# A graph network on one core: the first sort reads its partner keys in place, and the table's tiles are evacuated a step later

## The chip, the core and the metric

The kernel runs on one core of a Trainium2 chip. A core has TensorE (PE) for matrix products and transposes, VectorE (DVE), ScalarE (ACT) and GpSimd (POOL) for element-wise work, SyncE (SP) as a queue for DMAs, and 16 DMA engines. Each engine works through its own instructions in the order in which they were written down and waits for others by semaphores. SBUF is the working memory, PSUM the memory into which TensorE writes. The metric is the device time of the whole kernel in microseconds. Three runs took 4322.46, 4323.11 and 4330.8 us; the median is 4323.11 us.

## The reference: what is computed

There are 12500 nodes with 256 features each and 200000 edges, sorted by destination. The first layer normalises the features, multiplies them by a weight matrix, gathers a row of the product for each edge and adds it, times the edge's weight, to the edge's source node. The second layer is attention over the edges with 8 heads.

```python
h = relu(layernorm(x))
# layer 0: table = h @ W0 ; out[src] += edge_weight * table[dst]
x = x + segment_sum(edge_weight[:, None] * (h @ weight)[dst], src, 12500)
h = relu(layernorm(x))
# layer 1: q, k, v = projections of h; softmax of q[dst].k[src] over the edges of one dst
x = x + segment_sum(attn * v[src], dst, 12500) @ Wo.T + bo
```

## The kernel before

The edges come sorted by destination, while layer 0 adds up by source. So the kernel sorts them again on the chip. The edges are split into three blocks of 128 x 512 edges and a rest of seven groups of 512. A block's keys (source and destination packed in one 32-bit number) are a tile K of 128 x 512, and the edge weights are a tile of values (V in the code, `W` in the profile). `sort(b)` is a bitonic sort of one block, written as a generator that yields after each stage. A stage compares two halves of the keys: `a` and `c` are views of K, the lower and upper partner of each pair. It makes a mask m of 128 x 256 (L231), the minimum (L234) and the maximum (L235) into a new K, and moves the values by predicated copies with the mask (L241, or L238 and L239 in a stage that flips one half). All five are on VectorE. Ahead of them ScalarE copies the partner keys `c` into a PSUM tile kp (L224) and all values into a PSUM tile vp (L229). There are 129 stages in the first sort. In 6 of them the partner is another tile, just transposed by TensorE (`kp=kt`); the other 123 make the copy kp.

Block 0 is sorted alone, before any layer-0 sum can start. Beside it runs `hidden()`, a second generator, which makes the table HW = relu(layernorm(x)) @ W0, 98 tiles of 128 rows in chunks of four. For one tile the functions are stats (DVE, L561 and L562), root (ACT, L569, once per chunk), scale (DVE, L575 and L576, once per chunk), norm (GpSimd, L581), turn (PE transposes, L587), turned (ACT, L592, PSUM to SBUF), mult (PE, L598) and put (ACT, L604, PSUM to SBUF, and after four tiles the store of the chunk to HW by SP, L607). The list `fs` gives for each function the lag in steps behind stats, and its order is the order in which a step's instructions are written into the engines' queues. A chunk of x is loaded by SP (L541) when the chunk before it is at its second tile; three chunks have buffers.

The loop that joins the two is in `layer0`. In each step s it advances the sort by a stage, then hidden by a step. In step 3 it prepares the rest block. From step 18 it loads what the seven rest groups need, and after step 20 it advances `group_l0`, which builds one-hot matrices on DVE (L495 to L507), multiplies on PE (L511, L518), evacuates on ACT (L513, L519), and adds rows to a table in DRAM by indirect DMAs from GpSimd (L522). Two fills a step, 20 copies of a part of x into the first accumulator (L734) and five small zero rows (L1470), go out on SP until they are used up. The order on all engines is as written, by `manual_schedule`.

PSUM tiles that matter: `pt` has one buffer (turn writes it, turned frees it); `bank()` gives `pg` with two buffers, which mult, and in a rest group the one-hot product and both message products, share.

After the loop `load_s` gathers rows of HW by the sorted destinations dT (L285 makes dT on DVE, L630 is the gather on GpSimd), and the rest of layer 0, the other two sorts and layer 1 follow.

Of the kernel before, what the change touches and what calls it, by code (L numbers as in the profile page):

```python
# [64 lines left out]
def sblk(g):  # L65
    b = 0
    while g >= GS[b]:
        g -= GS[b]
        b += 1
    return b, g  # L70
# [7 lines left out]
class Gnn:  # L78
# [127 lines left out]
    def sort(self, b):  # L206
# [3 lines left out]
        def halves(v, flip):  # L210
            return v[:, :, 0], v[:, ::-1, 1] if flip else v[:, :, 1]

        def stage(d, flip=False, kp=None, vp=None, rows=False):
            nonlocal K
            e = d if rows else G // (2 * d)
            n = G // (2 * e)

            def pairs(t):
                return t.rearrange("p (n c m) -> p n c m", c=2, m=e)

            a, c = halves(pairs(K), flip)
            if kp is None:
                kp = tp.tile([P, G], F32, name="kp", bufs=1)[:, :G // 2].rearrange("p (n m) -> p n m", m=e)
                nc.scalar.copy(kp, c)  # L224
            else:
                kp = halves(pairs(kp), flip)[1]
            if vp is None:
                vp = tp.tile([P, G], F32, name="vp", bufs=1)
                nc.scalar.copy(vp, V)  # L229
            m = wp.tile([P, G // 2], I32, name="m").rearrange("p (n m) -> p n m", m=e)  # L230
            nc.vector.tensor_tensor(m, a, kp, op=ALU.is_gt)  # L231
            K = wp.tile([P, G], F32, name="K")
            lo, hi = halves(pairs(K), flip)
            nc.vector.tensor_tensor(lo, a, kp, op=ALU.min)  # L234
            nc.vector.tensor_tensor(hi, a, kp, op=ALU.max)  # L235
            v, p = pairs(V), pairs(vp)
            if flip:
                nc.vector.copy_predicated(v[:, :, 0], m, p[:, ::-1, 1])  # L238
                nc.vector.copy_predicated(v[:, ::-1, 1], m, p[:, :, 0])  # L239
            else:  # L240
                nc.vector.copy_predicated(v, m[:, :, None, :].to_broadcast([P, n, 2, e]), p[:, :, ::-1])  # L241
# [7 lines left out]
        for k in range(1, 10):  # L249
            stage(1 << (k - 1), True)  # L250
            yield
            for j in range(k - 2, -1, -1):
                stage(1 << j)
                yield
# [271 lines left out]
    def hidden(self):  # L526
        nc, wp, tp = self.nc, self.wp, self.tp
        nt = (N + P - 1) // P
        X, Y, T, M, R = {}, {}, {}, {}, {}
        nch = (nt + HC - 1) // HC  # L530
        chunks = list(range(nch - 2, nch)) + list(range(nch - 2))
        seq = [i for c in chunks for i in range(c * HC, min(nt, (c + 1) * HC))]

        def rows(t, c):
            n = min(HC * P, N - c * HC * P) // P
            return t[c * HC * P:(c * HC + n) * P].rearrange("(k p) d -> p k d", p=P), n

        def load(c):
            X[c] = wp.tile([P, HC, D], F32, name="xh", bufs=3)
            v, n = rows(self.i["x"], c)  # L540
            nc.sync.dma_start(X[c][:, :n], v)  # L541
            if N - (c * HC + n) * P < P and n < HC:
                nc.sync.dma_start(X[c][:N % P, n], self.i["x"][N - N % P:N])

        def tile_of(i):
            return divmod(i, HC) + (min(P, N - i * P),)

        def last(i):
            return i % HC == HC - 1 or i == nt - 1

        def stats(i):
            c, j, r = tile_of(i)
            if j == 0:
                M[c] = wp.tile([P, HC, 2], F32, name="mv4")
                if nt - c * HC <= HC:
                    nc.vector.memset(M[c], 1.0)
            k = chunks.index(c) + 1
            if j == 1 and k < nch:
                load(chunks[k])
            st = wp.tile([P, 6], F32, name="st")  # L560
            nc.vector.bn_stats(st[:r], X[c][:r, j])  # L561
            nc.vector.bn_aggr(M[c][:r, j], st[:r])  # L562
            T[i] = {}

        def root(i):
            c, j, r = tile_of(i)
            if last(i):
                R[c] = wp.tile([P, HC, 2], F32, name="sd4")
                nc.scalar.activation(R[c][:, :j + 1, 0], M[c][:, :j + 1, 1], AF.Sqrt, bias=self.eps)  # L569

        def scale(i):
            c, j, r = tile_of(i)
            if last(i):
                m, a = M[c][:, :j + 1], R[c][:, :j + 1]
                nc.vector.reciprocal(a[:, :, 0], a[:, :, 0])  # L575
                nc.vector.scalar_tensor_tensor(a[:, :, 1], m[:, :, 0], -1.0, a[:, :, 0], op0=ALU.mult, op1=ALU.mult)  # L576

        def norm(i):
            c, j, r = tile_of(i)
            h = T[i]["h"] = wp.tile([P, D], F32, name="h", bufs=3)  # L580
            nc.gpsimd.tensor_scalar(h[:r], X[c][:r, j], R[c][:r, j, 0:1], R[c][:r, j, 1:2], op0=ALU.mult, op1=ALU.add)  # L581

        def turn(i):
            r = tile_of(i)[2]
            pt = T[i]["pt"] = tp.tile([P, G], F32, name="pt", bufs=1)[:, :D].rearrange("p (k e) -> p k e", e=P)
            for k in range(2):
                nc.tensor.transpose(pt[:, k, :r], T[i]["h"][:r, k * P:(k + 1) * P], self.ident[:r, :r])  # L587

        def turned(i):
            r = tile_of(i)[2]  # L590
            ht = T[i]["ht"] = wp.tile([P, 2, P], F32, name="ht", bufs=3)
            nc.scalar.activation(ht[:, :, :r], T[i]["pt"][:, :, :r], AF.Relu)  # L592

        def mult(i):
            r = tile_of(i)[2]
            ph = T[i]["ph"] = self.bank()[:, :D]
            for k in range(2):
                nc.tensor.matmul(ph[:r], T[i]["ht"][:, k, :r], self.w0[:, k], start=(k == 0), stop=(k == 1))  # L598

        def put(i):  # L600
            c, j, r = tile_of(i)
            if j == 0:
                Y[c] = wp.tile([P, HC, D], F32, name="yh")
            nc.scalar.copy(Y[c][:r, j], T.pop(i)["ph"][:r])  # L604
            if j == HC - 1 or i == nt - 1:
                v, n = rows(self.HW, c)
                nc.sync.dma_start(v, Y[c][:, :n])  # L607
                if r < P:
                    nc.sync.dma_start(self.HW[N - r:N], Y[c][:r, n])

        load(chunks[0])
        q = HC + 1
        fs = ((turn, q + 1), (mult, q + 2), (norm, q), (scale, 1), (stats, 0), (root, 0), (turned, q + 1), (put, q + 2))
        for s in range(nt + q + 2):
            for f, k in fs:
                if 0 <= s - k < nt:
                    f(seq[s - k])
            yield
# [839 lines left out]
    def layer0(self):  # L1458
        tc, nc = self.tc, self.nc
        ET = mybir.EngineType  # L1460
        with tc.tile_pool(name="k0", bufs=1) as self.k0, tc.tile_pool(name="w0", bufs=2) as self.wp, \
# [23 lines left out]
            def fills(n):  # L1485
                for _ in range(n):
                    if fill:
                        fill.pop(0)()

            with tc.manual_schedule(engines={ET.SP, ET.PE, ET.DVE, ET.Activation, ET.Pool}):  # L1490
# [7 lines left out]
                s, gs, live = 0, [], None  # L1498
                while rest or live:
                    for f in list(rest):  # L1500
                        if next(f, self) is self:
                            rest.remove(f)
                    if s == 3:
                        self.prep_a(NPT)
                        self.prep_c(NPT)
                    if s == 18:
                        for g in range(NS, NS + 2):
                            self.load_l0(g)
                        gs = list(range(NS, NG))
                    if s > 20:  # L1510
                        if live is None and gs:
                            g = gs.pop(0)
                            live = self.group_l0(g)
                        if live is not None and next(live, self) is self:
                            live = None
                            if gs and gs[0] + 1 < NG:
                                self.load_l0(gs[0] + 1)
                    if s > 0:
                        fills(2)
                    s += 1  # L1520
# [7 lines left out]
                for t in range(NGS + 6):  # L1528
                    b, p = sblk(t) if t < NGS else (NPT, t - NGS)
# [130 lines left out]
```

## Time and profile before

| what | value |
|---|---|
| median of three runs | 4323.11 us |
| the profiled execution | 5571.24 us, of it a span of 5569.2 us |
| PE busy | 3863.3 us, 69% |
| DVE busy | 3443.4 us, 62% |
| POOL busy | 2921.8 us, 52% |
| ACT busy | 2172.3 us, 39% |
| mean granted TensorE clock | 0.819 of full speed |
| first gather of HW starts | 403.06 us after the start |

Times in the profile are of one execution with the profiler on. A row of the costliest groups gives line, engine, operation, the tiles written and read, their shapes, the count, the busy time and the mean duration in ns. A row of the timeline gives start and duration in us, and in brackets how long the engine had stood idle before it and who released it. The view of waits gives total, count and longest in us. A busy-time row of a stretch gives the busy microseconds of PE, of its weight loads, of DVE, ACT and POOL, then the granted clock, the mean busy share of the DMA engines and GB/s.

The costliest rows of the page that belong to sort and table:

```profile
L241 DVE COPY_PREDICATED W<-m,vp 128x512 f32<-128x512 int32 x317 | 229.7, 725 | 0.0
```

### The profile page before, as it was taken

Reading aid. Unit: us, or ns where it says so; the run is one execution under the profiler, and the core shown is the slowest. Engines: PE = TensorE matmul, PEld = TensorE weight load, DVE = VectorE, ACT = ScalarE, POOL = GpSimd, SP = SyncE. Lnnn points to the kernel's source line nnn. Section 1 sums busy time; section 2 is a strip of 40 time slices with the busy share of each in tenths; the row PEclk is TensorE's granted clock in tenths of the full one; section 3 lists DMA queues with packets and bytes.
Section 4 is the critical chain, followed back from the end, with each engine's and each line's share of the span. In section 5 each row is a group of like instructions: output and inputs, shape, how many; then the busy total and the mean of one; then the engine's idle time right before and its main releaser. Section 6 shows DMA issues by size and latency. Waiting matters only on the chain. (4 is left out here: it accounts for less than half of the span.)

```text
span 5569.2 us, 61840 instructions
## 1 busy us (share of the span) xinstructions
PE 3863.3 (69%) x14078; PEld 2557.5 (46%) x14078; DVE 3443.4 (62%) x7373; ACT 2172.3 (39%) x6027; POOL 2921.8 (52%) x3096
## 2 busy tenths in 40 slices
PE   4745677656667577777477767777777777677776
PEld 3532344334434344444255555555555555455554
DVE  7786777557666355555265556556666666566665
ACT  4452334223323122222144444444454444455453
POOL 2316655555555565666445555555555555555552
PEclk8777788778788799999677878788888888888888
DMA  6424456555555566666556666666676776666673
GB/s 180 96 66 141 146 164 181 167 161 162 164 157 168 156 201 197 201 194 192 173 172 196 190 199 203 201 193 206 197 213 208 208 214 208 201 207 210 202 213 105
DMA packets 627547, 1004.38 MB, mean 180 GB/s; under 512 B 97274, under 2 KB 450359, under 8 KB 627165
## 3 DMA queue, kind: packets, MB, share of 16 engines
q0 software_dynamic: 196224, 596.49, 38.0%
q1 hardware_dynamic: 430941, 403.79, 22.9%
q8 instruction: 119, 1.95, 0.2%
q14 instruction: 263, 2.15, 0.1%
HBM read 788.60 MB, written 224.47 MB: 182 GB/s over the span
## 5 line engine op out<-in xcount | busy, mean ns | idle before, releaser
L960 POOL DMA_INDIRECT kvt<-KV,ci x1564 | 1495.4, 956 | 1321.8 <-DVE pv L1059 666.3
L630 POOL DMA_INDIRECT hg<-HW,dT x1384 | 1311.5, 948 | 977.0 <-issue 369.3
L993 PE MATMUL pq<-qt,oht 80*128 80x256 f32 x3128 | 898.8, 435 | 395.5 <-issue 175.1
L650 PE MATMUL pg<-hg,ohs 128*128 128x256 f32 x2768 | 923.1, 454 | 134.4 <-issue 92.7
L994 DVE TENSOR_TENSOR pr<-pq,kvt 128x512 f32<-128x512 f32 x782 | 517.3, 686 | 796.2 <-remote 505.1
L1071 PE MATMUL pg<-pv,oh 128*82 128x264 f32 x3126 | 945.0, 455 | 67.6 <-DVE pv L1059 44.6
L993 PEld LDWEIGHTS pq<-qt,oht 80*128 80x128 f32 x3128 | 675.2, 220 | 564.4 <-issue 260.4
L650 PEld LDWEIGHTS pg<-hg,ohs 128*128 128x128 f32 x2768 | 549.6, 219 | 495.9 <-issue 370.9
L977 ACT ACTIVATE oh<-iof,nsl 128x82 f32<-128x82 f32 x1564 | 437.1, 350 | 855.5 <-remote 564.1
L1071 PEld LDWEIGHTS pg<-pv,oh 128*82 128x82 f32 x3126 | 556.4, 182 | 359.6 <-issue 163.0
L639 DVE TENSOR_SCALAR ohs<-iop,sT,eT 128x128 f32<-128x128 f32 x1384 | 473.2, 404 | 123.7 <-remote 74.8
L1059 DVE TENSOR_TENSOR pv<-kvt,pp 128x1024 f32<-128x1024 f32 x391 | 471.4, 1206 | 63.2 <-ACT pb L1048 43.5
L995 DVE TENSOR_REDUCE sim<-pr 128x32 f32<-128x1024 f32 x391 | 477.1, 1220 | 13.4
L649 PE MATMUL pg<-wn,cs 128*1 128x256 f32 x746 | 254.4, 427 | 196.5 <-ACT wn L671 73.1
L968 ACT ACTIVATE oht<-slt,npcol 80x512 f32<-80x512 uint8 x391 | 282.1, 722 | 257.2 <-remote 102.1
L671 ACT COPY wn<-pg 128x256 f32<-128x256 f32 x373 | 138.0, 370 | 384.0 <-PE pg L650 131.1
L465 ACT ACTIVATE sd<-mv,eps 128x1 f32<-128x1 f32 x128 | 37.7, 294 | 600.0 <-DVE sd L470 279.1
L697 PE MATMUL tps<-wkv,ht 128*128 128x512 f32 x512 | 262.5, 639 | 0.0
L969 ACT ACTIVATE oht<-oht 80x512 f32<-80x512 f32 x391 | 246.4, 630 | 12.4
L438 PE MATMUL pt<-w,ht 128*128 128x256 f32 x304 | 115.9, 468 | 173.5 <-ACT ht L435 146.0
L241 DVE COPY_PREDICATED W<-m,vp 128x512 f32<-128x512 int32 x317 | 229.7, 725 | 0.0
L443 DVE TENSOR_TENSOR xh<-pt,xh 128x256 f32<-128x256 f32 x152 | 64.4, 424 | 260.6 <-PE pt L438 141.6
(295 smaller groups left out, 4632.1 us busy)
## 6 DMA issues: line engine op xcount, KB each, us to landing
KV<-K SPq DMA_DIRECT2D x128, 256.0 KB
AG<-ag SPq DMA_DIRECT2D x391, 82.5 KB
tw<-acc SPq DMA_DIRECT2D x248, 128.0 KB
acc<-ws SPq DMA_DIRECT2D x248, 128.0 KB
qt<-Q SPq DMA_DIRECT2D x391, 80.0 KB
kvt<-KV,ci POOLq DMA_INDIRECT x1564
hg<-HW,dT POOLq DMA_INDIRECT x1384
xh<-acc SPq DMA_DIRECT2D x152, 128.0 KB
```

What stands on the lines that cost most here:

```text
L630: nc.gpsimd.indirect_dma_start(out=hg[:, w], out_offset=None, in_=self.HW, in_offset=bass.IndirectOffsetOnAxis(ap=self.part[b][0][:, c:c + ...
L639: self.nc.vector.tensor_scalar(oh[:, w], self.iop, sT[:, c], eT[:, c], op0=ALU.is_equal, op1=ALU.mult)
L650: nc.tensor.matmul(pg, oh[:, w], hg[:, w], start=(w == 0), stop=(w == n - 1))
L697: nc.tensor.matmul(X["kv"], X["ht"][:, k], self.wkv[:, k], start=(k == 0), stop=(k == 1))
L960: nc.gpsimd.indirect_dma_start(out=kv[:, w], out_offset=None, in_=self.KV, in_offset=bass.IndirectOffsetOnAxis(ap=self.csi[b][:, p, w:w + ...
L968: nc.scalar.activation(oht, sl, AF.Abs, bias=self.npcol[:QW])
L977: nc.scalar.activation(oh[:, w], self.iof[:, :MA], AF.Abs, bias=self.nsl[b][:, p, w:w + 1])
L993: nc.tensor.matmul(pq[:, c], oht[:, 2 * a + c], qt, start=True, stop=True)
L994: nc.vector.tensor_mul(pr[:, 2 * a:2 * a + 2], pq, kv[:, 2 * a:2 * a + 2, :D])
L995: nc.vector.tensor_reduce(sim[:, :, i, :], pr.rearrange("p w (h d) -> p w h d", h=H), op=ALU.add, axis=AX.X)
L1059: self.nc.vector.tensor_tensor(pv[:, :, :D].rearrange("p w (h d) -> p w h d", h=H), kv[:, :, D:].rearrange("p w (h d) -> p w h d", h=H), s ...
L1071: nc.tensor.matmul(pg, oh[:r, w], pv[:r, w], start=(w == 0), stop=(w == nw - 1))
```

## The change

In the first sort (b == 0) a stage no longer copies the partner keys: kp is the view `c` of K itself, in SBUF. The values are still copied, and the other two sorts are as before. In `hidden` the functions turned and put are moved to the head of a step and lag one step more, so that a tile's transposes and its product are evacuated in the step after the one in which TensorE makes them; root comes last in a step. The loop runs one step longer. In the joining loop hidden is advanced only in steps with s * 85 mod 100 below 85, 17 of 20, so that the 106 steps of hidden end at step 124 of some 130. The rest groups' loads move from step 18 to 24 and their work from after step 20 to after step 28.

```diff
             a, c = halves(pairs(K), flip)
-            if kp is None:
+            if kp is None and b == 0:
+                kp = c
+            elif kp is None:
                 kp = tp.tile([P, G], F32, name="kp", bufs=1)[:, :G // 2].rearrange("p (n m) -> p n m", m=e)
                 nc.scalar.copy(kp, c)
...
-        fs = ((turn, q + 1), (mult, q + 2), (norm, q), (scale, 1), (stats, 0), (root, 0), (turned, q + 1), (put, q + 2))
-        for s in range(nt + q + 2):
+        fs = ((turned, q + 2), (put, q + 3), (turn, q + 1), (mult, q + 2), (norm, q), (scale, 1), (stats, 0), (root, 0))
+        for s in range(nt + q + 3):
...
-                        if next(f, self) is self:
+                        if (f is self.KS or s * 85 % 100 < 85) and next(f, self) is self:
                             rest.remove(f)
...
-                    if s == 18:
+                    if s == 24:
...
-                    if s > 20:
+                    if s > 28:
```

## The prediction, made before the changed kernel had run

> **What bounds the kernel now.** The page's chain of waits covers only the last microsecond, so I began where the change acts: the first stretch, in which the first sort and the making of the table HW run side by side. Its end is found from the first gather of HW (L630, GpSimd), which needs the sorted destinations: the line view of L630 and the busy time of the stretch 0 to 402.4 us say
>
> ```profile
>   DVE dT L285: 51.0, 1
> 0.00:402.40 402.40, 219.38 (x820) 159.94 (x820) 311.26 (x951) 200.28 (x507) 100.73 (x134) 0.76 0.42 114
> ```
>
> GpSimd stood idle for 51.0 us until VectorE had dT, the last product of the sort, at 402.4 us. Everything later hangs on that instant, so a microsecond off the sort is a microsecond off the kernel. The second line lists PE, weight loads, DVE, ACT, POOL: DVE is busy 311.3 of 402.4 us, no other engine over 220. DVE sets the stretch, and what can be won is its 91 us of idle time. The view of waits of this stretch names it (total, times, longest):
>
> ```profile
> DVE m L231 <- ACT kp L224: 67.8, 38, 6.3
> DVE df L174 <- DMA di<-in_dst: 4.6, 1, 4.6
> DVE st L561 <- DMA xh<-in_x: 3.7, 1, 3.7
> DVE m L231 <- ACT K L274: 3.6, 6, 1.3
> ```
>
> So 67.8 us is the compare (L231) waiting for ScalarE's copy of the partner keys (L224). The timeline shows two kinds. The common one, every fourth step:
>
> ```profile
> 78.61 0.42 DVE L561 BATCH_NORM_STATS2 st<-xh 128x6 f32<-128x256 f32 x1
> 79.33 0.30 ACT L569 ACTIVATE sd<-mv,eps 128x4 f32<-128x4 f32 x1 [2.12 <-DVE mv L562]
> 79.54 0.36 ACT L592 ACTIVATE ht<-pt 128x256 f32<-128x256 f32 x1
> 79.80 0.36 ACT L604 COPY yh<-pg 128x256 f32<-128x256 f32 x1
> 80.05 0.39 ACT L224 COPY kp<-K 128x256 f32<-128x256 f32 x1
> 80.47 0.42 DVE L231 TENSOR_TENSOR m<-K,kp 128x256 int32<-128x256 f32 x1 [1.24 <-ACT kp L224]
> ```
>
> The square root waits for DVE's statistics; two evacuations and then the key copy stand behind it on ACT, and DVE loses 1.24 us. I count 18 such stalls of 1.15 to 1.25 us, 22 us together. The rare kind comes with an edge group of `group_l0`:
>
> ```profile
> 141.84 3.78 PE L518 MATMUL pg<-hw,ct 128*128 128x256 f32 x8 [0.68 <-ACT ct L513]
> 143.95 0.59 ACT L519 COPY ms<-pg 128x512 f32<-128x512 f32 x1 [2.16 <-PE pg L518]
> 145.66 0.59 ACT L519 COPY ms<-pg 128x512 f32<-128x512 f32 x1 [1.12 <-PE pg L518]
> 146.57 0.42 DVE L231 TENSOR_TENSOR m<-K,kp 128x256 int32<-128x256 f32 x1 [6.35 <-ACT kp L224]
> ```
>
> There are 7 of these, 1.9 to 6.4 us long, 29 us together. The rest: 5.5 us once at 70.27 us (ACT held by a full HW store), 5.0 us in three start-up waits (2.63, 1.69, 0.63), and some 10 us around the transposes.
>
> **The change, part by part.**
>
> *The key copy goes.* 123 copies of 0.385 us leave ACT (47 us, not the bound). On DVE no instruction leaves: m, min and max stay. What goes is the wait ahead of m; next late is the value copy vp (L229, 0.59 us), which only the predicated copy (L241) needs, three instructions or 1.0 us after m starts (start to start 0.33 us: 399.19 to 400.18 in the pure sort steps). In a root stall, with the root now last, vp starts right behind it: the root's successor starts 0.21 us after 79.33, so vp would end at about 80.13; m, min and max fill 79.23 to 80.22. The stall goes whole: 18 x 1.24 = **22 us**. In pure sort steps nothing changes: vp ends 0.27 us ahead of its user there already. At the transposes, the five row stages whose K comes from DVE's own multiplication (L259) lose 0.55 to 1.07 us each, 4.3 us, and four late evacuations 1.7 us: **6 us**. The stages that compare with the transposed tile (kp=kt) keep their 3.6 us.
>
> *The evacuations move to the head of the next step.* turned and put then find TensorE's work of the step before done; put's waits on PE (34.8 us of ACT's time in this stretch) mostly vanish. When PE is slow a tile takes 0.69 + 1.91 us, when fast 0.41 + 1.03, on average 1.9 by the busy time of L587 and L598 over 98 tiles, against 2.4 us per tile in the spread schedule (17 steps of 2.12 us and 3 of 1.60 for 17 tiles). It keeps up. The price is in the edge groups: `bank` has two slots; the tile's product now holds one until the next step, so the two products of a group share the other, and the second product waits for ScalarE's copy of the first. In the built instruction streams the second L518 pair now waits on Activation instead of PE. That adds a copy, 0.59 us, and two hand-overs, about 0.95 us per group, while the early compare gives back about 0.75 us (the predicated copy can follow vp's start by 0.68 instead of kp's by 1.43). Per group 0.2 us worse: **-1.4 us**, and the 29 us stay.
>
> *The spread, 17 table steps in 20.* DVE's sum is unchanged. But early SP work is reordered: the load of the third chunk of x stands behind six table fills (L734) after 34.6 us instead of four, the next behind twelve instead of eight, while the x loads and fills share DMA engines busy 100% from 40 to 70 us. A fill is 0.64 MB, 1.9 us at the 340 GB/s of that time. The first load lands about 3.8 us later than its 47.2 us, less what SP gains, so DVE waits some 6.5 us instead of 3.7; the next costs about 3.6 us where none was. Against it the 5.5 us at 70.27 us go (the HW store is issued four steps ahead of the buffer's next use instead of three) and 2.2 us of the start-up waits. Together **+1.3 us**. At the end, the last HW store is issued about 5.5 us before dT (three pure steps of 1.60 and dT's own 0.4), and the last store before landed 3 us after its issue (DMA busy to 363.5 us), so the first gather still waits for dT: 0. Should it not fit, 1 to 2 us. The groups' later start (step 28 for 20) is free: they end near step 70 of 130.
>
> Sum: 22 + 6 - 1.4 + 1.3 = **28 us** before the next point.
>
> *The compares now have two SBUF inputs.* The duration alone costs nothing: L397, both inputs from one SBUF tile, took 0.30 us for 151 elements, L375 0.51 for 360, the same line on which 0.415 for 256 lies. The risk is GpSimd, which normalises the table tiles (L581, 0.55 us, x98) beside the sort. The Trainium skill (SBUF — State Buffer, "Who interferes with whom") speaks against this change: a VectorE instruction with two SBUF inputs and a GpSimd instruction that reads SBUF lock each other out, and the second to come blocks until the first is done. The trace has two-input operations beside L581, in the edge groups:
>
> ```profile
> 159.00 2.63 POOL L581 TENSOR_SCALAR h<-xh,sd 128x256 f32<-128x256 f32 x3
> 159.59 1.09 DVE L495 TENSOR_TENSOR S<-sr,c 128x512 f32<-128x512 int16 x1
> 160.92 0.32 DVE L502 SCALAR_TENSOR_TENSOR scr<-S,lower 128x128 f32<-128x128 f32 x1
> 162.04 0.28 DVE L502 SCALAR_TENSOR_TENSOR scr<-S,lower 128x128 f32<-128x128 f32 x1
> ```
>
> L495 takes 0.66 us alone, 1.09 here; L502 takes 0.28 alone and 0.32 beside L581. So the lock is there, but mostly brief. Over the 28 L502 and 7 L495 the excess over their clean times adds to about 1.85 us, with some 23 L581 around: 0.08 us for each. In those pieces two-input operations are 43% of DVE's time, in a sort step 47%. By the row: 98 x 0.08 x 47/43 = 9 us. By the rule, with each L581 a full block: 98 x 0.55 = 54 us; with the chance that it starts ahead of a compare (about half) and a loss of 0.4 as in L495, 20 us. Below nothing it can't go. I take **9 us**, nearest the row, and keep 2 and 54.
>
> Net: 28 - 9 = **19 us**. The profiled execution took 5571.24 us (span 5569.2, 2 us around it), so it would take 5552. It is 1248 us above the median of 4323.11. I take the saving over in full, since this stretch is made of DVE instructions whose spacing follows their size; if profiling stretched it like the whole (1.289), 15 us remain. So 4323 - 19 = **4304 us**.
>
> **Rivals.**
> - *The lock decides (slower).* Place: L581 against L231, L234, L235, bursts of two to four right after the scale. Price 0.55 us each; it eats the whole gain from 28 / 98 = 0.29 us per L581, and at the full price gives 28 - 54 = -26: 4349 us. For it: the rule, and L495's +0.43. Against: most L502 lost 0.03.
> - *vp takes the place of kp (no change).* If ACT is still late by over 1 us at most steps, because slow PE delays turned and put, the predicated copy waits where the compare did. For it: vp stands behind the same evacuations. Against: they now wait for a step-old product. It would leave 0 to 8 us: about 4320.
> - *More than the sum.* If lock and early loads cost almost nothing and the edge groups' chain shortens too (in the 6.35 us case TensorE had stood 4.2 us for h, which a step of slack partly hides), 28 + 12 = 40 us: 4283.
> - The change not doing what it says is ruled out: 123 ACT copies are gone from the built streams.
>
> **Chances and range.** My forecast (gain of 9 to 34 us) 0.50, more 0.14, no change 0.20, slower 0.16. 0.2% is 8.6 us. Faster 0.64, same 0.20, slower 0.16. The range takes the larger gain to 43 us and, on the other side, a loss of 7: 4280 to 4330.
>
> **What would show it.** dT (L285) at about 383 us instead of 402.4; no wait of m for ACT except the kp=kt stages; new waits of the predicated copy only at the seven edge groups, 3 to 6 us each; x waits near 50 and 62 us; m, min and max at 0.41 us with a tail up to 0.8 beside L581. I am wrong if these three average over 0.5 us, if the predicated copy waits for vp in ordinary steps, or if the first gather waits for the HW store.

## The result and the profile after

| | before | after |
|---|---|---|
| median on the chip of the prediction, 20 runs each | 4320.53 us (4305.28 to 4330.95) | 4300.81 us (4288.36 to 4323.53) |
| ratio of the times, with its 95% interval | | 0.9959 [0.9946, 0.9972] |
| profiled execution | 5571.24 us, span 5569.2 | 4297.47 us, span 4295.4 |
| start of dT, the sort's last product | 402.4 us | 379.9 us |

The change makes the kernel faster by 0.4%, 12 to 23 us, and the forecast was 4304.0 us. The two profiled executions can't be set against each other as wholes: they come from different chips, which the section on the hardware takes up. The first stretch can, to about 4 us (the changed kernel's dT came at 379.9 us on one chip and at 383.9 on another), and it is where the change acts. First, in the profile after, who waits for dT at the first gather of HW (total, times), and the busy time up to dT (PE, its weight loads, DVE, ACT, POOL, clock, DMA share, GB/s):

```profile
  DVE dT L287: 16.9, 1
0.00:379.90 379.90, 203.13 (x820) 145.15 (x820) 315.94 (x950) 158.69 (x384) 116.47 (x134) 0.84 0.44 121
```

The gather still waits for dT alone. DVE is busy for 315.9 us of 379.9, where it was 311.3 of 402.4. So its idle time fell from 91.1 to 64.0 us, by 27.2 before rounding, its work grew by 4.7, and dT comes 22.5 us earlier. The view of DVE's waits in this stretch (total, times, longest) says what is left of the idle time:

```profile
DVE W L243 <- ACT vp L231: 28.0, 10, 6.8
DVE st L563 <- DMA xh<-in_x: 10.3, 2, 5.5
DVE m L233 <- ACT K L276: 6.6, 5, 2.8
DVE df L174 <- DMA di<-in_dst: 4.6, 1, 4.6
DVE K L261 <- PE tps L248: 4.2, 5, 1.1
DVE W L240 <- ACT vp L231: 1.8, 1, 1.8
```

The 67.8 us in which the compare waited for the key copy are gone, and 29.8 us of the predicated copies (L243 and L240) waiting for the value copy vp have come. Of these 25.1 us lie in the seven edge groups, 2.7 in two steps of the start-up (1.84 at 16 us, 0.90 at 35 us), 1.8 in a step at 260 us in which TensorE was late because h was, and 0.2 near the end. The second line is the price of the table fills standing ahead of two loads of x: 10.3 us for 3.7. The third, the stages that compare with a transposed tile, has grown from 3.6 to 6.6 us.

A step with a root, in the timeline after (start, duration, engine, line):

```profile
72.66 0.39 DVE L233 TENSOR_TENSOR m<-K 128x256 int32<-128x256 f32 x1
72.84 0.30 ACT L571 ACTIVATE sd<-mv,eps 128x4 f32<-128x4 f32 x1 [0.76 <-DVE mv L564]
72.97 0.41 DVE L236 TENSOR_TENSOR K<-K 128x256 f32<-128x256 f32 x1
73.04 0.58 ACT L231 COPY vp<-W 128x512 f32<-128x512 f32 x1
73.31 0.42 DVE L237 TENSOR_TENSOR K<-K 128x256 f32<-128x256 f32 x1
73.65 0.74 DVE L243 COPY_PREDICATED W<-m,vp 128x512 f32<-128x512 int32 x1
```

The root is followed by vp at once. Since vp (73.04 + 0.58) ends as the maximum does, the predicated copy starts with no wait in brackets. The stall of 1.24 us that stood here is gone whole.

An edge group, in the same timeline:

```profile
125.45 1.55 POOL L524 DMA_INDIRECT acc<-ms,idx  x1 [3.49 <-DMA acc<-ms,idx]
126.49 2.14 POOL L583 TENSOR_SCALAR h<-xh,sd 128x256 f32<-128x256 f32 x3
127.66 0.69 PE L589 MATMUL pt<-ident,h 128*128 128x128 f32 x2 [4.42 <-POOL h L583]
131.63 0.58 ACT L515 COPY ct<-pg 128x512 f32<-128x512 f32 x1 [7.71 <-PE pg L513]
132.26 1.13 PE L520 MATMUL pg<-hw,ct 128*128 128x256 f32 x4 [0.68 <-ACT ct L515]
133.43 0.58 ACT L521 COPY ms<-pg 128x512 f32<-128x512 f32 x1 [1.22 <-PE pg L520]
134.07 1.13 PE L520 MATMUL pg<-hw,ct 128*128 128x256 f32 x4 [0.68 <-ACT ms L521]
135.72 0.60 ACT L231 COPY vp<-W 128x512 f32<-128x512 f32 x1
136.35 0.73 DVE L243 COPY_PREDICATED W<-m,vp 128x512 f32<-128x512 int32 x1 [6.76 <-ACT vp L231]
```

The second product (134.07) now waits for ScalarE's copy of the first, as foretold, because only one slot of `bank` is free. But look at 131.63 first: ScalarE stood 7.71 us for the one-hot product L513. That wait is not the bank's. TensorE had been idle for 4.42 us before L589 at 127.66, waiting for h from GpSimd (L583), and L513 is queued behind that tile's transposes and product. GpSimd was late because its norm stands behind the group's indirect DMAs in its queue: one that started at 125.45 us had waited 3.49 us for the DMA before it.

What the compares cost beside GpSimd, in the groups view of this stretch (count, then busy us, mean ns, idle ahead of it), the mask of before first:

```profile
L231 DVE TENSOR_TENSOR m<-K,kp 128x256 int32<-128x256 f32 x123 | 49.9, 405 | 68.7 <-ACT kp L224 67.8
L233 DVE TENSOR_TENSOR m<-K 128x256 int32<-128x256 f32 x123 | 54.1, 440 | 0.2
L236 DVE TENSOR_TENSOR K<-K 128x256 f32<-128x256 f32 x123 | 52.0, 423 | 0.0
L237 DVE TENSOR_TENSOR K<-K 128x256 f32<-128x256 f32 x123 | 51.7, 420 | 0.0
```

Mask, minimum and maximum took 405, 415 and 415 ns before. The growth is 4.2 + 1.0 + 0.7 = 5.9 us over the 98 norms, 0.06 us for each. That is VectorE's side. GpSimd's side is larger: its norm, before and after (fastest, median and slowest in ns, then the first start and the last):

```profile
L581 POOL TENSOR_SCALAR h<-xh,sd x98: 547/556/1564, 38.4 to 351.5; 128x256 f32<-128x256 f32 x97, 84x256 f32<-84x256 f32 x1
L583 POOL TENSOR_SCALAR h<-xh,sd x98: 549/817/1870, 38.3 to 363.1; 128x256 f32<-128x256 f32 x97, 84x256 f32<-84x256 f32 x1
```

The median norm is 0.26 us longer (by the means 0.12: 782 and 900 ns). It comes with the reading in place and not with the order: 1089 ns where only the copy goes (copy_only below), 555 where only the order changes (order_only).

### The profile page after: what moved, and what is told of

Its sections match the earlier page's. It is cut to its first block, busy times and chain, and to the rows that moved or that the text cites. A ratio compares the mean times of both kernels' runs of the same rounds, so it can differ in the third digit from the quotient of the medians.

```text
span 4295.4 us, 61707 instructions
## 1 busy us (share of the span) xinstructions
PE 3436.9 (80%) x14078; PEld 2287.8 (53%) x14078; DVE 3436.4 (80%) x7373; ACT 2132.2 (50%) x5904; POOL 2942.4 (69%) x3096
## 5 line engine op out<-in xcount | busy, mean ns | idle before, releaser
L652 PE MATMUL pg<-hg,ohs 128*128 128x256 f32 x2768 | 877.8, 424 | 190.7 <-DMA hg<-HW,dT 80.2
L1073 PE MATMUL pg<-pv,oh 128*82 128x264 f32 x3126 | 840.3, 416 | 71.3 <-DVE pv L1061 60.9
L652 PEld LDWEIGHTS pg<-hg,ohs 128*128 128x128 f32 x2768 | 476.6, 198 | 582.9 <-issue 217.9
L995 PE MATMUL pq<-qt,oht 80*128 80x256 f32 x3128 | 766.1, 388 | 8.7 <-ACT oht L971 7.4
L995 PEld LDWEIGHTS pq<-qt,oht 80*128 80x128 f32 x3128 | 609.0, 196 | 117.7 <-ACT oht L971 9.1
L1073 PEld LDWEIGHTS pg<-pv,oh 128*82 128x82 f32 x3126 | 497.5, 164 | 317.7 <-issue 80.5
L996 DVE TENSOR_TENSOR pr<-pq,kvt 128x512 f32<-128x512 f32 x782 | 516.7, 684 | 162.6 <-PE pq L995 87.4
L243 DVE COPY_PREDICATED W<-m,vp 128x512 f32<-128x512 int32 x317 | 228.3, 720 | 28.0 <-ACT vp L231 28.0
L231 ACT COPY vp<-W 128x512 f32<-128x512 f32 x344 | 203.2, 591 | 92.2 <-DVE W L243 70.9
L699 PE MATMUL tps<-wkv,ht 128*128 128x512 f32 x512 | 241.4, 594 | 0.0
L651 PE MATMUL pg<-wn,cs 128*1 128x256 f32 x746 | 229.7, 390 | 2.1 <-ACT wn L673 2.1
L721 DVE TENSOR_TENSOR K<-tps,bias 128x512 f32<-128x512 f32 x128 | 88.6, 692 | 174.9 <-PE tps L699 167.5
```

Source lines behind the costliest of these rows:

```text
L652: nc.tensor.matmul(pg, oh[:, w], hg[:, w], start=(w == 0), stop=(w == n - 1))
L995: nc.tensor.matmul(pq[:, c], oht[:, 2 * a + c], qt, start=True, stop=True)
L996: nc.vector.tensor_mul(pr[:, 2 * a:2 * a + 2], pq, kv[:, 2 * a:2 * a + 2, :D])
L1073: nc.tensor.matmul(pg, oh[:r, w], pv[:r, w], start=(w == 0), stop=(w == nw - 1))
```

## The experiments

All ran on other chips than the one of the prediction, chips on which the kernel before takes 5545.52 us (67 runs; the first four experiments), 5545.84 us (57 runs; the next four) and 5539.73 us (45 runs; the last four). Each ratio is against the kernel before on the same chip. The instant of dT (402.4 us before, 379.9 after) is read from one profile each, so differences of some 4 us between kernels mean little.

**The parts alone.** One edit is made to the kernel before, without the other.

```diff
# copy_only, against before
-            if kp is None:
+            if kp is None and b == 0:
+                kp = c
+            elif kp is None:
```

> The key copy alone goes; order of the evacuations, lag and spread are those of before. My theory (the copy is what VectorE waited for, and the order only shortens what is left): the root stall shrinks from 1.24 to about 0.5 us of waiting by the predicated copy, x18 = -13; the groups' stalls lose 0.75 each, -5; transposes -6; start -2; contention with GpSimd +6. dT at about 381 us, 4301 us. Rival (the value copy takes the place of the key copy as long as the order is the old one): dT above 395 us, 4315 us or more.

dT at 391.0 us; time 5542.77 us, 0.9992 [0.9977, 1.0008]. Waits of DVE:

```profile
DVE W L243 <- ACT vp L231: 35.3, 25, 5.7
DVE W L240 <- ACT vp L231: 12.6, 4, 5.4
```

dT gains 11.4 us, half of the whole. The wait has moved rather than gone: 25 times DVE now stands before the predicated copy of L243, 16 times of these for 0.47 us at a root, since in the old order two evacuations still stand between root and vp. The groups keep 30.3 us, where they cost 29.2: I had given them 0.75 us each for the early compare, and it did not show.

```diff
# order_only, against before
-        fs = ((turn, q + 1), (mult, q + 2), (norm, q), (scale, 1), (stats, 0), (root, 0), (turned, q + 1), (put, q + 2))
-        for s in range(nt + q + 2):
+        fs = ((turned, q + 2), (put, q + 3), (turn, q + 1), (mult, q + 2), (norm, q), (scale, 1), (stats, 0), (root, 0))
+        for s in range(nt + q + 3):
```

> The copy stays, turned and put are moved to the head of the next step with the root last; no spread, groups at their old steps. My theory: the key copy starts 0.42 us earlier in a root stall, x18 = -8, but the groups' second product waits for the copy of the first, +7, late evacuations -2: dT at about 399 us, 4317 us. Rival (the order is what gains, since it takes ScalarE's waits for TensorE away): dT at 385 us or below.

dT at 392.4 us, 10.0 earlier; time 5540.66 us, 0.9994 [0.9982, 1.0006].

```profile
DVE m L231 <- ACT kp L224: 47.9, 34, 6.0
DVE st L561 <- DMA xh<-in_x: 8.0, 2, 4.4
```

The order shortens the stalls on the key copy by itself, from 67.8 to 47.9 us (a root stall is 0.70 us now), and it alone brings the second wait for x. The groups wait for 25.9 us here, although their two products share one slot of `bank` in this order. In time neither part can be told from the kernel before: both intervals include 1.

```diff
# order_spread, against after: the order and the spread, with the key copy
-            if kp is None and b == 0:
-                kp = c
-            elif kp is None:
+            if kp is None:
```

> Everything of the change but the reading in place: the copy of the partner keys stays. My theory: as the order alone, with two waits for tiles of x of about 5 us each that the spread brings and the 5.5 us wait for the full HW store gone: dT at about 401 us, 4319 us, no difference from before. Rival (spread and order gain by themselves): dT at 390 us or below.

dT at 401.3 us; time 5548.98 us, 1.0005 [0.9992, 1.0018].

```profile
DVE m L231 <- ACT kp L224: 55.2, 39, 7.9
```

With the copy kept, spreading the table costs 8.9 us against the order alone: the waits for kp are 7.3 us more, and the stages with a transposed tile wait 9.4 us where they waited 6.1.

```diff
# no_spread, against after: the copy gone, the new order, groups at their old steps
-                        if (f is self.KS or s * 85 % 100 < 85) and next(f, self) is self:
+                        if next(f, self) is self:
...
-                    if s == 24:
+                    if s == 18:
...
-                    if s > 28:
+                    if s > 20:
```

> Reading in place and the new order, without the spread and with the groups at their old steps. My theory: the waits for x fall from 10.3 to about 4 us, the wait for the full HW store comes back in part: dT between 376 and 382 us, 4298 to 4303 us, no different from the full change. Rival (the spread is what gives TensorE room): dT above 388 us.

dT at 381.5 us; time 5532.47 us, 0.9977 [0.9964, 0.9989].

```profile
DVE W L243 <- ACT vp L231: 20.3, 7, 6.3
DVE st L563 <- DMA xh<-in_x: 11.1, 2, 6.4
```

The two edits add up, as far as single profiles tell: 11.4 + 10.0 = 21.4 us apart, 20.9 together. And with both, no root is left at which DVE waits for vp. The spread adds nothing to them that one profile could tell (381.5 here, 379.9 and 383.9 in two profiles of the changed kernel). The longer waits for x are no work of the spread either: they are here too, at 46 and 71 us instead of 50 and 64.

**The changed kernel on such a chip**, no edit.

> The changed kernel itself, to have its trace on the same chip as the parts. My theory: dT at 380 us within 2 us whatever the chip, since the stretch is made of VectorE instructions; saving about 20 us of the time. Rival (the 22 us between the two traces come from a faster chip, not from the change): dT at 390 us or more on a chip on which the kernel before takes 5545 us.

dT at 383.9 us; time 5539.86 us, 0.9986 [0.9973, 0.9998].

```profile
DVE W L243 <- ACT vp L231: 31.6, 11, 6.0
DVE st L563 <- DMA xh<-in_x: 10.1, 2, 5.3
L233 DVE TENSOR_TENSOR m<-K 128x256 int32<-128x256 f32 x123 | 54.3, 442 | 0.2
```

The first stretch repeats to 4 us. The saving in time, 8 us with an interval of 1 to 15, is smaller than the 18.5 us of dT. It is not lost before the third sort ends. The rows of dT in before and in this run (fastest, median and slowest in ns, then the first start and the last) put its last start 26 us earlier:

```profile
L285 DVE TENSOR_SCALAR dT<-K x3: 402/421/463, 402.4 to 1801.9; 128x512 int32<-128x512 int32 x3
L287 DVE TENSOR_SCALAR dT<-K x3: 410/419/463, 383.9 to 1775.9; 128x512 int32<-128x512 int32 x3
```

Part of this may be that before's one profile was a late one: its 5571.24 us stand 25 to 32 us above the three medians of that kernel, and the control below, which is that kernel with idle work added to GpSimd, had dT at 397.8 us. Counted from 397.8 instead of 402.4, dT's gain here is 13.9 us. The rest is open.

**What the lock costs.** A second norm per tile is put on GpSimd, 98 more operations into a tile that nothing reads; in the changed kernel, and as a control in the kernel before, whose compares have one input in PSUM.

```diff
# after_norm2 and before_norm2, against after and before
             nc.gpsimd.tensor_scalar(h[:r], X[c][:r, j], R[c][:r, j, 0:1], R[c][:r, j, 1:2], op0=ALU.mult, op1=ALU.add)
+            g = wp.tile([P, D], F32, name="hh", bufs=1)
+            nc.gpsimd.tensor_scalar(g[:r], X[c][:r, j], R[c][:r, j, 0:1], R[c][:r, j, 1:2], op0=ALU.mult, op1=ALU.add)
```

> The changed kernel with the table's normalisation done twice on GpSimd, the second time into a tile that nothing reads: 98 more GpSimd instructions of 0.55 us that read SBUF beside the compares. By the row (0.06 us lost by VectorE for each): dT 5 to 8 us later than the changed kernel. By the full lock (0.55 us each): dT about 50 us later.

> The same doubling in the kernel before, whose compares have one input in PSUM: the control. GpSimd is idle most of this stretch, so both theories expect dT within 3 us of 402.4; if it is much later, the doubling costs by GpSimd's own time and not by the lock.

Changed kernel: dT at 390.5 us, 6.6 later than without; time 5537.9 us, 0.9988 [0.9970, 1.0006]. Control: dT at 397.8 us, not later than before; 1.0001 [0.9983, 1.0018]. The mask's row in the groups view, first of the changed kernel with two norms, then of the control:

```profile
L233 DVE TENSOR_TENSOR m<-K 128x256 int32<-128x256 f32 x123 | 58.5, 476 | 0.2
```

```profile
L231 DVE TENSOR_TENSOR m<-K,kp 128x256 int32<-128x256 f32 x123 | 49.9, 406 | 63.2 <-ACT kp L224 60.8 <-ACT ht L594 1.2
```

With two norms beside it the two-input mask goes from 442 to 476 ns, its worst instance to 1547; with kp in PSUM it stays at 406. GpSimd shows the same from its side: the added norm has a median of 560 ns in the control and of 1024 ns in the changed kernel. So the slowdown is real and goes with the second SBUF input. Of the 6.6 us 4.5 are VectorE's own busy time (316.4 to 320.9 us), 0.05 us for each added GpSimd operation and not 0.55; the other 2.1 us are longer waits, no more than two profiles of one kernel differ by. Only the mask grows: minimum and maximum, with two SBUF inputs as well, stay at 422 and 421 ns (424 and 418 with one norm). Why the first of the three takes it was not tried.

**The shared PSUM slot.** The second message product of a group is put into the PSUM tile kp, which block 0 no longer uses.

```diff
# bank3, against after
-            pm = self.bank().rearrange("p (c d) -> p c d", d=D)
+            pm = (self.tp.tile([P, G], F32, name="kp", bufs=1) if a else self.bank()).rearrange("p (c d) -> p c d", d=D)
```

> The changed kernel with the second message product of a rest group put into the PSUM tile that the first sort no longer uses for partner keys, so that it needn't wait for ScalarE's copy of the first product. My theory: 0.95 us less at each of 7 groups, dT about 6 us earlier than the changed kernel, 374 us. Rival (the group's chain is set by TensorE and h, not by the shared buffer): dT within 1.5 us of the changed kernel.

dT at 384.8 us, so nothing is gained there and the rival held. The timeline of the same group:

```profile
132.77 2.08 PE L520 MATMUL pg<-hw,ct 128*128 128x256 f32 x4 [0.67 <-ACT ct L515]
134.64 1.91 PE L520 MATMUL kp<-hw,ct 128*128 128x256 f32 x4
137.70 0.73 DVE L243 COPY_PREDICATED W<-m,vp 128x512 f32<-128x512 int32 x1 [7.78 <-ACT vp L231]
```

The second product no longer waits. But four matmuls take 2.08 and 1.91 us here, where they took 1.13 in the changed kernel, and the predicated copy starts no earlier. TensorE was that slow in five of the seven groups of this run, and in two in the changed kernel on the same chip. So the run doesn't tell what the slot is worth at equal TensorE speed. The time, 5526.11 us and 0.9964 [0.9951, 0.9977], is better than that of the changed kernel beside it, though dT is not; I have no explanation for that.

**Three edits that go at what is left.** One table fill a step instead of two, so that the loads of x stand behind fewer:

```diff
# fills1, against after
-                        fills(2)
+                        fills(1)
```

> The changed kernel with one table fill a step instead of two on SP, so that the loads of x stand behind half as many fills. My theory (the two waits for x, 10 us, come from the order on SP): they fall to 3 us or less, dT 7 us earlier, at about 377 us. Rival (the DMA engines are full anyway, and the load waits wherever it stands): the waits stay above 8 us.

dT at 377.9 us; time 5515.28 us, 0.9966 [0.9951, 0.9981]. The waits for x, 10.1 us, are gone; dT gains only 6.0 of them, as the groups wait longer (32.9 us in all for 27.9 in the changed kernel on the slower kind of chip):

```profile
DVE W L243 <- ACT vp L231: 34.0, 9, 6.9
DVE m L233 <- ACT K L276: 6.2, 5, 2.4
```

The norm is moved from GpSimd to ScalarE (with the Relu that its consumer applies anyway, so the table is unchanged):

```diff
# norm_act, against after
-            nc.gpsimd.tensor_scalar(h[:r], X[c][:r, j], R[c][:r, j, 0:1], R[c][:r, j, 1:2], op0=ALU.mult, op1=ALU.add)
+            nc.scalar.activation(h[:r], X[c][:r, j], AF.Relu, bias=R[c][:r, j, 1:2], scale=R[c][:r, j, 0:1])
```

> The changed kernel with the table's normalisation on ScalarE (with its relu) instead of GpSimd: no GpSimd instruction reads SBUF beside the compares but the indirect DMAs, and h no longer stands behind them in GpSimd's queue. My theory: compares back at 0.41 us, 5 to 6 us; the groups' chains start earlier, 3 to 8 us; ScalarE has room (161 of 382 us busy, 36 more). dT at about 373 us. Rival (ScalarE's queue is what the predicated copy waits for, so another instruction in it costs more than the lock): dT at 386 us or later.

dT at 368.8 us, more than expected; time 5504.69 us, 0.9943 [0.9929, 0.9958]. The mask's row and the wait for vp:

```profile
L233 DVE TENSOR_TENSOR m<-K 128x256 int32<-128x256 f32 x123 | 49.3, 400 | 0.2
DVE W L243 <- ACT vp L231: 21.0, 9, 5.8
```

Both effects of GpSimd's norm go at once: the mask is back at 400 ns (slowest 445), and the groups wait 19.6 us instead of 27.9. Of the 15.1 us of dT 9.0 are VectorE's busy time (316.4 to 307.5 us) and 6.1 its waits. That the groups gain because h no longer stands behind their indirect DMAs is argued: h is also free of GpSimd's own slowdown here, and no run parts the two.

The two together, and the three:

```diff
# both: fills1 and norm_act; both_bank3: these and bank3
```

> Both: one fill a step and the normalisation on ScalarE. My theory: the two gains add, dT at about 366 us, and the time about 15 us below the changed kernel's. Rival (what is taken away here comes back as another wait on ScalarE or TensorE): dT above 375 us.

> Both, and the second message product of a group in the tile of the unused key copy. With h no longer late, the shared buffer may set the chain: my theory 3 to 6 us less than both alone, dT at 361 to 363 us. Rival (TensorE's speed in the group sets it, as it did with this edit alone): within 1.5 us of both.

dT at 357.1 us and 349.0 us, each better than expected; times 5494.72 and 5495.62 us (7 runs each), 0.9939 [0.9916, 0.9961] and 0.9939 [0.9917, 0.9961]. The wait for vp and the busy time up to dT with all three:

```profile
DVE W L243 <- ACT vp L231: 13.9, 8, 4.5
0.00:349.00 349.00, 202.04 (x820) 144.54 (x820) 307.28 (x950) 204.10 (x482) 45.27 (x36) 0.86 0.46 132
```

The PSUM edit, worth nothing alone, goes with 8 us of dT here. Of these 4.8 are waits for vp (18.7 in `both`); 3.2 are waits around the transposes, which the edit doesn't touch. That with h on time the group's chain from one product to the next ends last is one reading; the other is that TensorE ran the products of five groups fast here (1.13 and 1.03 us), and of only two in bank3. DVE's idle time is 41.7 us, of 91.1 in the kernel before. These two beat both kernels of this case, by some 34 us (22 to 46) over before, measured on the chip of 5540 us only (over the changed kernel, which ran on another chip, by the ratios alone); against each other they can't be told apart in time.

## Why the prediction was right

**The bound.** dT was to come at about 383 us and came at 379.9 and 383.9. The first gather waits for dT in both kernels, and not for the HW store. But that a microsecond off the sort is a microsecond off the kernel did not hold: in every run but bank3 the time gained less than dT did, the most in `both_bank3` (53.4 us of dT, 34 of time). Part of this may again be before's late profile.

**The root stalls and the copy, 22 + 6 us.** Right in sum, and shown by the root step above. That the credit went to the copy's removal was too simple: it takes 11.4 us alone, the new order alone takes 10.0, and only with both does vp follow the root in time. The transposes' share is off: the other waits there are gone, but the term "keep their 3.6 us" measured 6.6 us, and the waits for TensorE at the key multiplication went from 2.7 to 4.2. That is 4.5 us worse than foretold.

**The edge groups, -1.4 us.** Predicted 29 + 1.4 = 30.4 us; measured 25.1 and, on another chip, 27.9. The hand-over through the shared slot is there, but the price put on it does not show: order_only has it and waits 25.9 us where before waited 29.2, and bank3, which takes it away, won nothing, though with a slower TensorE. The 0.75 us credited to the early compare did not come in copy_only. What the sum of the prediction left out is that h is late (it stood only among the rivals): with the norm on ScalarE (norm_act) the groups wait 8.3 us less. The other 19.6 us have no shown cause.

**The spread and the loads of x, +1.3 us.** The x waits were put at 6.5 us near 50 and 3.6 near 62, 10.1 in sum. They are 5.5 at 50.1 and 4.7 at 63.8 us, and the 5.5 us at 70 are gone. But the cause named was in part wrong: no_spread has two waits of this size as well, 4.7 and 6.4 us, so they come with the new order.

**The lock, -9 us.** The mechanism held and the size on VectorE was 5.9 us (0.06 for each norm where 0.08 was taken). The row of L502, mostly 0.04 us longer beside the norm, was the right guide. The Trainium skill's rule (SBUF — State Buffer, "Who interferes with whom"), by which the second to come waits until the first is done, makes 54 us of it only if VectorE is always the second. The prediction priced GpSimd's side at nothing, and there the trace has more: the median norm went from 556 to 817 ns. What the rule would do to VectorE at its worst nearly occurs: one mask took 822 ns, 0.42 us over its usual 0.40, where a norm takes 0.55.

**The sum.** DVE's idle time fell by 27.2 us where 28 were foretold, its busy time grew by 4.7 where 9 were, so dT gained 22.5 us for 19. The time gained 17.7 us by the ratio, 12 to 23. That it lies so near the 19 is in part luck: dT came 3.5 us better than foretold, and on the slower chips only 8 (1 to 15) of 18.5 us of dT showed in the time. None of the rivals came: the lock did not decide, vp did not take kp's place in ordinary steps (4.7 us outside the groups, 2.7 of them at the start), and 40 us off dT needed edits that the change doesn't make.

**Where it failed.** The step "if profiling stretched it like the whole (1.289)" rested on nothing. The kernel before takes some 5545 us on the chips of the experiments, and the changed kernel's profiled execution, 4297.47 us, lies among its 20 runs on the chip of the result. So 5571 us is the time of another chip, and profiling did not stretch it by 1248 us. It did no harm because the first stretch is nearly the same on both kinds of chip (dT at 379.9 and 383.9 us). The prediction had a reason for taking the saving over in full, VectorE's instructions, but for another case than the one that it was in.

## What to carry to other kernels

When a copy that an engine waits for is taken away, ask what stands in front of the next thing on the same queue: here the removal paid in full only once the evacuations behind the root had been moved as well. A rule that two engines block each other says that a cost exists; its size comes from a row in which both already run side by side, and here it was a ninth of a full block for VectorE. The other engine's row belongs to the price too: here GpSimd's norm grew by more than the compares did. And a wait is worth following upstream past the engine that is named: ScalarE was named for the groups' 25 us, TensorE stood behind it, and GpSimd's late norm behind both, where one moved instruction won more than the PSUM slot that the timeline pointed to.

## What the hardware showed that I had not expected

Chips differ. The busy row and the granted clock of the changed kernel's page, on the chip of the result (first fence) and on a chip of the experiments (second):

```profile
PE 3436.9 (80%) x14078; PEld 2287.8 (53%) x14078; DVE 3436.4 (80%) x7373; ACT 2132.2 (50%) x5904; POOL 2942.4 (69%) x3096
```

```profile
PE 3868.2 (70%) x14078; PEld 2558.7 (46%) x14078; DVE 3449.7 (62%) x7373; ACT 2131.7 (38%) x5904; POOL 2949.0 (53%) x3096
```

The same instructions take the same time on DVE, ACT and POOL, and TensorE's take 12.6% more. Its mean granted clock was 0.923 in the first and 0.821 in the second, and the matmul of L995 took 388 and 441 ns on average. Its median is 379 ns on both, so the second chip reaches the same speed and is slow more often. The whole took 4297.47 and 5542.34 us. That is 1245 us, far more than the 431 us of TensorE's own busy time, and it lies behind the first stretch, in which the clock was 0.84 on both (0 to 380 us). What makes the rest of it is open, and so is whether the lower clock is a cause or comes of the waits. The waits differ too: on the second chip the view names a releaser "remote", which it doesn't explain, 83 times ahead of L996 alone (527.9 us), and on the first chip never. So a profile and a table of times can come from different chips, and a cost behind the first stretch should not be carried from one to the other.
